# A transformer sandwich on one core: the last chunk's experts in pieces of two, one and one blocks

## The chip, the cores and the metric

The kernel runs on one core of a Trainium2 chip. Time is device microseconds of one execution; the number compared is the median over runs. The profile is one further execution, taken by the hardware profiler, with its own time.

## What is computed

Four sequences of 1024 tokens with 128 channels (fp32) pass through four residual layers, each `x = x + layernorm(layer(layernorm(x)))`: a linear recurrence (RWKV), a mixture of 16 experts, a delta-net attention, and last the layer this change is about:

```python
def _gqa(x, wq, wk, wv, wo):          # 16 heads of 8, 4 key heads, causal
...
    attn = jnp.where(causal, attn, jnp.float32(-jnp.inf))
    attn = jax.nn.softmax(attn, axis=-1)
    out = jnp.einsum('bhqk,bkhd->bqhd', attn, v).reshape(B, S, C)
    return out @ wo.T
def _moe(x, gate_w, expert_w):        # 8 experts, top 2, softmax of the two
    logits = t @ gate_w.T
    w, sel = jax.lax.top_k(logits, TOP_K)
...
    for e in range(N_EXPERTS):
        out = out + comb[:, e, None] * (t @ expert_w[e].T)
h = x + _gqa(_rmsnorm(x, attn_norm_w), wq, wk, wv, wo)
out = h + _moe(_rmsnorm(h, ffn_norm_w), gate_w, expert_w)
```

## The kernel before

Channels lie on the 128 partitions and tokens along the free axis, in chunks of 512 tokens (CH); a sequence is two chunks (NH) or eight blocks of 128 (NBLK). Stages A to C (the first three layers) run first, their later sequences interleaved with the last stage. The last stage is one long list written in the order in which the engines are to take it, with the scheduler switched off (`tc.manual_schedule()`): each engine works through its own instructions in just that order and waits where an operand isn't there.

The loop at the end walks over blocks (b, i), sequence by sequence. For each it issues units. A unit of `weighted` (L925) is one TensorE matmul of 128 keys against 4 heads by 128 queries (sc, L945, 512 columns), and its Exp on ScalarE (pr, L950); on the diagonal GpSimd masks pr (L954). Eight units behind, `products` (L937) multiplies four pr by the values into av, which holds 32 rows for each group of heads: eight sums, the denominator in row 8. Block i has 4(i + 1) such units. Between them lie the units of `maxima` of the block two ahead (matmul sm, L874 to L886, and a maximum on VectorE, L882 and L887), so the last two blocks, (3, 6) and (3, 7), with 28 and 32 units, have none beside them. The row maxima go into extra rows of qr by small DMAs (L909). sc has two PSUM banks (`scores`), sm three (`to_max`), av one.

After each unit comes `tick()`. A tick issues what is due, half a step of the work ahead (stage C and heads of the next sequences), and 0.65 step (PER_TICK_BEHIND) of the oldest generator in `behind_it`. A step is what a generator issues up to its next `yield`:

```python
        owed[1] = min(owed[1] + PER_TICK_BEHIND, 1.5)
        if behind_it and owed[1] >= 1.0:
            owed[1] -= 1.0
            if next(behind_it[0], True):
                behind_it.popleft()
```

These generators are `experts(b, h)`, one for each chunk, put there once its fourth block has its av. `finish` copies av (L964) to SBUF and stores its sums to DRAM (L971). `experts` first calls `project_out`: den and num come back from DRAM, heads spread over the partitions (L985, L986), Ln and Exp turn den into its reciprocal (L988, L989), GpSimd multiplies (L992), TensorE projects (wo, L997). Then rmsnorm (L526, L138, L120, L121, L1011), gate logits with tokens on partitions (L1016), top 2 on VectorE (L145 to L163, L1019 to L1029, L176 to L180), a transpose to 8 rows (comb, L1037), a store of them (row, L1044) and eight loads that spread each expert's row over 128 partitions (every, L1050). GpSimd forms n4 times gate for each expert (share, L1062), and TensorE adds the eight experts up (y, L1074), with the term of the residual centered ahead (L1057). Layernorm (L1076, L526, L138, L120, L121, L1081), residual (L1083), transposes back (L1088), the means (L1091) and the store of the output (L1094) follow. One such generator has about 80 steps. At the very end a loop of ticks drains what is left.

Of the kernel before, what the change touches and what calls it, by code (L numbers as in the profile page):

```python
# [11 lines left out]
FP = mybir.dt.float32  # L12
BF = mybir.dt.bfloat16
AF = mybir.ActivationFunctionType
# [4 lines left out]
P = 128  # L19
NB = 4  # L20
# [19 lines left out]
def sandwich(ctx: ExitStack, tc: tile.TileContext, x, vecs, cmats, rope, wa, wb, wc, wd, out):  # L40
# [73 lines left out]
    def chunk(h):  # L114
        return slice(h * CH, (h + 1) * CH)
# [20 lines left out]
    def project(pp, lhsT, rhs, name):  # L136
        ps = pp([P, CH], name)
        nc.tensor.matmul(ps, lhsT=lhsT, rhs=rhs, start=True, stop=True)  # L138
        return ps

    def topk(vals, nb, n_e, k, restart, pool):
# [21 lines left out]
        nc.vector.tensor_add(sel, sel, eq)  # L163
        return sel

    def restarts(nb, n_e, pool, name):
# [353 lines left out]
    def wait_for_it():  # L520
        for _ in range(LAG):
            yield

    def mean_square_steps(pp, src):
        sq = pp.scratch("rs")
        nc.scalar.activation(sq, src, AF.Square)  # L526
        yield
        yield
        ps = project(pp, mean, sq, "ln_v")
        yield  # L530
        return ps
# [393 lines left out]
    def weighted(b, i):  # L925
# [36 lines left out]
        def finish():  # L962
            av = pd.tile([P, CH], FP, tag="avs", name="av_sb")
            nc.scalar.copy(av, pavs.pop((b, i)))  # L964
            if i % 4 == 0:
                sums[b, i // 4] = dram.tile([4, 4, 9, CH], FP, tag="sums", name="sums")
            to = sums[b, i // 4].rearrange("g r d t -> g d r t")

            def stored():
                for g in range(4):  # L970
                    nc.sync.dma_start(out=to[g][:, :, tb], in_=r3(av[32 * g : 32 * g + 9, :], 4))  # L971
                if i % 4 == 3:
                    behind_it.append(experts(b, i // 4))

            later_on(4, stored)

        return [lambda j=j, g=g: unit(j, g) for j in range(i + 1) for g in range(4)]

    def project_out(b, h):

        n3, of = n3s[b, h], sums.pop((b, h))
        num = pd.tile([P, CH], FP, tag="share", name="num", bufs=3)
        den = pd.tile([P, CH], FP, tag="every", name="den", bufs=4)
        heads_of = of.rearrange("g r d t -> (g r) d t")
        nc.sync.dma_start(out=den, in_=heads_of[:, 8:9].to_broadcast([16, 8, CH]))  # L985
        nc.sync.dma_start(out=num, in_=heads_of[:, 0:8])  # L986
        yield from wait_for_it()
        nc.scalar.activation(den, den, AF.Ln)  # L988
        nc.scalar.activation(den, den, AF.Exp, scale=-1.0)  # L989
        yield  # L990
        yield
        nc.gpsimd.tensor_mul(num, num, den)  # L992
        yield
        yield
        yield
        po = room_f([P, CH], "wo_ps")
        nc.tensor.matmul(po, lhsT=wo_d, rhs=num, start=True, stop=True)  # L997
        nc.vector.tensor_add(n3, po, n3)
        yield

    def experts(b, h):

        yield from wait_for_it()
        yield from project_out(b, h)
        c = chunk(h)
        hT = n3s[b, h]
        n4 = pd.tile([P, CH], FP, tag="n4", name="n4", bufs=1)
        var = yield from mean_square_steps(room_f, hT)
# [4 lines left out]
        yield  # L1013
        pg = room_f([P, 4, 8], "gate_ps")
        for n in range(4):
            nc.tensor.matmul(pg[:, n, :], lhsT=n4[:, n * P : (n + 1) * P], rhs=wgate_d, start=True, stop=True)  # L1016
        yield
        lg = pd.tile([P, 4, 8], FP, name="lg")
        nc.vector.tensor_copy(lg, pg)  # L1019
        yield  # L1020
        sel = topk(lg, 4, 8, 2, restart8, pd)
        top = pd.tile([P, 4, 1], FP, name="top")
        nc.vector.tensor_reduce(top, lg, AX.X, ALU.max)
        nc.vector.tensor_sub(lg, lg, top.to_broadcast([P, 4, 8]))
        yield
# [3 lines left out]
        nc.vector.tensor_mul(sel, sel, lg)  # L1029
        normalized(sel, 4, 8, 0.0, pd)  # L1030
        yield
        yield
        yield

        pt = room_f([8, CH], "comb_ps")
        for n in range(4):
            nc.tensor.transpose(pt[:, n * P : (n + 1) * P], sel[:, n, :], ident)  # L1037
        yield
        comb = pd.tile([8, CH], FP, tag="last", name="comb", bufs=1)
        nc.scalar.copy(comb, pt)  # L1040
        yield
        yield
        row = dram.tile([8, CH], FP, tag="row", name="row")
        nc.sync.dma_start(out=row, in_=comb)  # L1044
# [3 lines left out]
        def spread_gate():  # L1048
            every = pd.tile([P, CH], FP, tag="every", name="every", bufs=4)
            nc.sync.dma_start(out=every, in_=row[len(gates)].partition_broadcast(P))  # L1050
            gates.append(every)
# [3 lines left out]
        yield from wait_for_it()  # L1055
        y = room_f([P, CH], "y")
        nc.tensor.matmul(y, lhsT=center, rhs=hT, start=True, stop=False)  # L1057
        shares = []

        def weigh():  # L1060
            shares.append(pd.tile([P, CH], FP, tag="share", name="share", bufs=3))
            nc.gpsimd.tensor_mul(shares[-1], n4, gates[len(shares) - 1])  # L1062
# [22 lines left out]
        yield  # L1085
        px = room_f([P, 4, P], "x_t")
        for j in range(4):
            nc.tensor.transpose(px[:, j, :], n4[:, j * P : (j + 1) * P], ident)  # L1088
        yield
        last = pd.tile([P, 4, P], FP, tag="last", name="last", bufs=1)  # L1090
        nc.vector.tensor_add(last, px, means[:, b, h * 4 : h * 4 + 4].unsqueeze(2).to_broadcast([P, 4, P]))  # L1091
        for _ in range(4):
            yield
        nc.sync.dma_start(  # L1094
            out=out[b, h * CH : (h + 1) * CH, :].rearrange("(n p) c -> p n c", p=P), in_=last,
        )
        yield

# [32 lines left out]

    coming = front()
    PER_TICK, PER_TICK_BEHIND = 0.5, 0.65
    owed = [0.0, 0.0]

# [4 lines left out]
    def tick():  # L1140
# [8 lines left out]
        if owed[0] >= 1.0:  # L1149
            owed[0] -= 1.0  # L1150
            advance()
        owed[1] = min(owed[1] + PER_TICK_BEHIND, 1.5)
        if behind_it and owed[1] >= 1.0:
            owed[1] -= 1.0
            if next(behind_it[0], True):
                behind_it.popleft()

    for h in range(NH):
# [13 lines left out]
    wexp = pd.tile([P, 8, P], FP, name="wexp", bufs=1)  # L1172
    nc.sync.dma_start(out=wexp, in_=wd[:, 328:].rearrange("p (e o) -> p e o", e=8))
    centered(wexp, 8, pd, "wmean")
    with tc.manual_schedule():
# [4 lines left out]
        for n, (b, i) in enumerate(blocks):  # L1180
# [9 lines left out]
            while (b, i) not in placed_rows:  # L1190
                tick()
            for u in units_of(n):
                u()
                tick()
        while held:
            held[0][0]()
            tick()
        while due or behind_it:
            tick()


def _constants():
# [13 lines left out]
    for p in range(P):  # L1216
        rope[p, 0] = cos[p % 4]
        rope[p, 1] = sin[p % 4] if p % 8 >= 4 else -sin[p % 4]
    return cmats, rope.reshape(P, -1)


def _arrays(i):

    cmats, rope = _constants()
    a = {n: np.asarray(v) for n, v in i.items()}
# [23 lines left out]
    def by_d(w):  # L1249
# [4 lines left out]
        by_d(a[F1 + "wq"].T), by_d(a[F1 + "wk"].T), a[F1 + "wv"].T, a[F1 + "wo"].T, a[F1 + "gate_w"].T,  # L1254
        a[F1 + "expert_w"].reshape(1024, P).T,
    ]
# [22 lines left out]
```

## Time and profile before

| | |
|---|---|
| runs, us | 1712.28, 1715.19, 1717.48; median 1715.19 |
| profiled execution, us | 1715.55, its span 1713.8 |
| busy, share of the span | PE 1310.6 (76%), DVE 1168.9 (68%), ACT 856.7 (50%), POOL 655.9 (38%) |
| last attention product (av) | starts at 1659.13, its copy at 1661.95 to 1662.54 |
| last store issued | 1710.60 |
| granted TensorE clock | 1.00 from 1600 to 1660, 0.68, 0.63 and 0.80 after it |

A line of the timeline is: start, duration, engine, source line, operation, out<-in with shapes, how many in a row were merged, and in brackets how long the engine had been idle and who ended that. An fp32 matmul appears as two passes (x2). PEld is the load of the weights. A line of the chain is: start, duration, engine, what. SPq rows are DMA issues on SyncE's queue.

### The profile page before, as it was taken

Reading aid. Unit: us, or ns where it says so; the run is one execution under the profiler, and the core shown is the slowest. Engines: PE = TensorE matmul, PEld = TensorE weight load, DVE = VectorE, ACT = ScalarE, POOL = GpSimd, SP = SyncE. Lnnn points to the kernel's source line nnn. Section 1 sums busy time; section 2 is a strip of 40 time slices with the busy share of each in tenths; the row PEclk is TensorE's granted clock in tenths of the full one; section 3 lists DMA queues with packets and bytes.
Section 4 is the critical chain, followed back from the end, with each engine's and each line's share of the span. In section 5 each row is a group of like instructions: output and inputs, shape, how many; then the busy total and the mean of one; then the engine's idle time right before and its main releaser. Section 6 shows DMA issues by size and latency. Waiting matters only on the chain.

```text
span 1713.8 us, 15167 instructions
## 1 busy us (share of the span) xinstructions
PE 1310.6 (76%) x4593; PEld 463.3 (27%) x4604; DVE 1168.9 (68%) x1991; ACT 856.7 (50%) x1565; POOL 655.9 (38%) x663
## 2 busy tenths in 40 slices
PE   2547887867865889678779869888887879889864
PEld 1213333312221323133223223322232223233311
DVE  4575676698775877867995597777779825577601
ACT  3457776624453457234436625645553345645561
POOL 5554353524252324323433363427227333122212
PEclk8669998978887999877779869987898669989996
DMA  2000110313033122101112111231113011110101
GB/s 97 13 7 6 25 50 25 96 40 108 13 111 110 53 65 85 44 12 34 45 58 70 53 57 54 70 92 46 38 37 101 21 48 64 45 61 29 54 22 56
DMA packets 59330, 90.49 MB, mean 53 GB/s; under 512 B 9904, under 2 KB 26800, under 8 KB 58544
## 3 DMA queue, kind: packets, MB, share of 16 engines
q1 hardware_dynamic: 59248, 89.52, 17.3%
q8 instruction: 36, 0.59, 0.1%
q14 instruction: 46, 0.38, 0.1%
HBM read 76.38 MB, written 12.71 MB: 52 GB/s over the span
## 4 chain that ended last, share of the span: by engine, by line
PE 32%; DVE 18%; ACT 6%; issue 4%; POOL 4%; DMA 2%; SPq 0%; POOLq 0%; DVEq 0%; ACTq 0%
PE av L937 8%; PE sc L945 5%; DVE ms L882 4%; DVE st L620 4%; ACT pr L950 3%; PE sm L874 3%; DVE ms L887 3%; PE y L1074 3%; PE sm L886 2%; PE ln_v L138 2%; PE num_ps L674 1%; POOL hid L473 1%; POOL share L1062 1%; PE sm L878 1%; PE g_ps L138 1%
## 5 line engine op out<-in xcount | busy, mean ns | idle before, releaser
L950 ACT ACTIVATE pr<-sc 128x512 f32<-128x512 f32 x576 | 328.2, 595 | 361.7 <-PE sc L945 358.0
L882 DVE TENSOR_REDUCE ms<-sm 128x1 f32<-128x512 f32 (+3 forms) x352 | 210.5, 633 | 114.2 <-PE sm L878 103.0
L945 PE MATMUL sc<-qr,keys_r 75*128 75x512 bf16 x576 | 234.1, 422 | 37.7 <-ACT pr L950 28.7
L887 DVE TENSOR_REDUCE ms<-sm 128x1 f32<-128x512 f32 x256 | 165.0, 682 | 56.4 <-PE sm L886 55.9
L937 PE MATMUL av<-pr,va 128*32 128x512 f32 x1152 | 183.1, 710 | 0.0
L954 POOL TENSOR_SCALAR_AFFINE_SELECT pr<-pr 128x512 f32<-128x512 f32 x128 | 89.4, 712 | 244.5 <-ACT pr L950 236.2
L874 PE MATMUL sm<-keys_r,qr 72*128 72x512 bf16 (+3 forms) x512 | 138.2, 337 | 46.3 <-DVE ms L882 43.9
L138 PE MATMUL ln_v<-rs,cm 128*128 128x512 f32 x176 | 113.0, 733 | 43.0 <-ACT rs L126 28.3
L473 POOL TENSOR_TENSOR hid<-hid,gate 128x512 f32<-128x512 f32 x64 | 81.9, 1280 | 162.9 <-DVE hid L468 124.6
L614 POOL TENSOR_TENSOR kv<-vrep,phi 128x512 f32<-128x512 f32 x64 | 85.6, 1342 | 115.0 <-issue 47.9
L1062 POOL TENSOR_TENSOR share<-n,every 128x512 f32<-128x512 f32 x64 | 87.2, 1373 | 91.1 <-DMA every<-row 70.5
L455 PE MATMUL y_ps<-hid,wbt 128*128 128x512 f32 x144 | 84.1, 669 | 46.3 <-DVE hid L474 44.4
L886 PE MATMUL sm<-keys_r,qr 72*128 72x512 bf16 x256 | 99.6, 417 | 25.0 <-DVE ms L887 20.6
L945 PEld LDWEIGHTS <-keys_r 75*128 75x128 bf16 x576 | 58.7, 106 | 153.2 <-issue 126.3
L878 PE MATMUL sm<-later,identb 128*128 128x128 bf16 (+2 forms) x341 | 90.5, 265 | 0.0
L474 DVE TENSOR_TENSOR hid<-hid,g 128x512 f32<-128x512 f32 x72 | 57.7, 801 | 46.7 <-POOL hid L473 39.9
L138 PE MATMUL u_ps<-n,wbt 128*128 128x512 f32 x144 | 77.3, 618 | 7.6 <-DVE hid L468 5.1
L138 PE MATMUL g_ps<-n,wbt 128*128 128x512 f32 x144 | 78.8, 630 | 3.7 <-DVE hid L463 1.6
L1074 PE MATMUL y<-share,wexp 128*128 128x512 f32 x128 | 70.8, 644 | 9.6 <-POOL share L1062 9.4
L874 PEld LDWEIGHTS <-qr 72*128 72x128 bf16 x512 | 51.0, 107 | 99.4 <-issue 82.8
L465 ACT ACTIVATE g<-hid 128x512 f32<-128x512 f32 x72 | 45.1, 626 | 55.4 <-DVE hid L463 55.3
L674 PE MATMUL num_ps<-st,cm 128*32 128x512 f32 x128 | 52.5, 777 | 25.7 <-DVE st L637 25.5
(300 smaller groups left out, 2394.9 us busy)
## 6 DMA issues: line engine op xcount, KB each, us to landing
gate<-rows SPq DMA_DIRECT2D x64, 256.0 KB
vrep<-v_rows SPq DMA_DIRECT2D x64, 256.0 KB
every<-row SPq DMA_DIRECT2D x64, 256.0 KB
qr<-dq SPq DMA_DIRECT2D x72, 128.0 KB
turn<-in_rope_dram SPq DMA_DIRECT2D x8, 512.0 KB
dq<-qp SPq DMA_DIRECT2D x8, 384.0 KB
keys_r<-dk SPq DMA_DIRECT2D x72, 32.0 KB
sums<-av_sb SPq DMA_DIRECT2D x128, 18.0 KB
```

What stands on the lines that cost most here:

```text
L138: nc.tensor.matmul(ps, lhsT=lhsT, rhs=rhs, start=True, stop=True)
L473: nc.gpsimd.tensor_mul(a, a, gate)
L874: nc.tensor.matmul(view[:, k, :], lhsT=qr[0:KROWS, h, tb], rhs=kr[0:KROWS, half, h // 4, 0:n_s], start=(k == 0), stop=False, skip_group_ch ...
L878: nc.tensor.matmul(view[:, :, n_s - P :], lhsT=identb, rhs=later[:, :in_bank, :], start=False, stop=True, skip_group_check=True,)
L882: nc.vector.tensor_reduce(ms[:, 0, h0 : h0 + in_bank], view, AX.X, ALU.max)
L886: nc.tensor.matmul(sc, lhsT=qr[0:KROWS, h, tb], rhs=kr[0:KROWS, 0, h // 4, :], start=True, stop=True)
L887: nc.vector.tensor_reduce(ms[:, 1, h : h + 1], sc, AX.X, ALU.max)
L937: nc.tensor.matmul(pavs[b, i][32 * g : 32 * g + 32, :], lhsT=va[:, j, g, :], rhs=pr, start=(j == 0), stop=(j == i),)
L945: nc.tensor.matmul(sc, lhsT=kr[0:ROWS, j // 4, g, j % 4 * P : (j % 4 + 1) * P], rhs=qr[0:ROWS, 4 * g : 4 * g + 4, tb], start=True, stop=True,)
L950: nc.scalar.activation(pr, sc, AF.Exp)
L1062: nc.gpsimd.tensor_mul(shares[-1], n4, gates[len(shares) - 1])
L1074: nc.tensor.matmul(y, lhsT=wexp[:, e, :], rhs=shares[e], start=False, stop=(e == 7))
```

## The change

Only the last chunk, blocks 4 to 7 of sequence 3, is treated in another way.

- Blocks 4 and 5 go through `experts` as one piece of 256 tokens; every tile of the generator is cut to `wide = nb * P` columns. It is put into `behind_it` after block 5.
- Blocks 6 and 7 (`LAST`) each have their own generator `last_block`, of 128 tokens, which every tick advances by one step, whatever the rate. It works without DRAM: eight matmuls with a new 0/1 constant `pick` lay the numerators and denominators of the heads out over the partitions; TensorE spreads a gate row with a matmul of a one-hot row block (`space["one"]`) against comb; VectorE multiplies four experts at once out of PSUM; shares are the stationary side and the expert weights the moving one, so that y has tokens on its partitions, the sum of squares comes from ScalarE's Square itself, and no transposes are needed at the end. x is transposed back and the means added ahead of that.
- `last_block` takes its PSUM tiles from `to_max`, and y from `scores`. Its SBUF lies in the buffer of qr of the chunk that is done.
- In sequence 3, blocks 4 to 7, the generators behind run at 1.0, 1.0, 2.0 and 2.0 steps a tick instead of 0.65.
- The constants `pick` (128 x 304 fp32) are appended to the weights and loaded once, behind wexp.

```diff
+                if (b, i) in LAST:
+                    later_on(1, lambda: ends.append(last_block(b, i, av)))
+                    return
...
-                if i % 4 == 3:
-                    behind_it.append(experts(b, i // 4))
+                if i % 4 == 3 or (b, i + 1) in LAST:
+                    behind_it.append(experts(b, i // 4, i % 4 + 1))
...
+    LAST = {(NB - 1, NBLK - 2), (NB - 1, NBLK - 1)}
+    def last_block(b, i, av):
+        if not space:
+            space["all"] = pe.tile([P, 32, P], FP, tag="qr", name="space")
+            space["one"] = space["all"][0:8, 24:32, :]
+            nc.vector.tensor_copy(space["one"], ident[0:8, 0:8].unsqueeze(2).to_broadcast([8, 8, P]))
...
+        px = to_max([P, P], "x_t")
+        nc.tensor.transpose(px, xT[b][:, c], ident)
+        parts = to_max([P, 2, P], "parts_ps")
+        for m in (1, 0):
+            for r in range(4):
+                nc.tensor.matmul(
+                    parts[:, m, :], lhsT=pick[:, m, 24 - 8 * r : 24 - 8 * r + P], rhs=av[:, r * P : (r + 1) * P],
+                    start=(r == 0), stop=(r == 3), skip_group_check=True,
+                )
+        nc.vector.tensor_scalar_add(xfin, px, means[:, b, i : i + 1])
+        yield
+        nc.scalar.activation(den, parts[:, 1, :], AF.Ln)
+        nc.scalar.activation(den, den, AF.Exp, scale=-1.0)
+        yield
+        nc.vector.tensor_mul(num, parts[:, 0, :], den)
+        yield
+        po = to_max([P, P], "wo_ps")
+        nc.tensor.matmul(po, lhsT=wo_d, rhs=num, start=True, stop=True)
+        yield
+        nc.vector.tensor_add(hT, po, hT)
...
+        nc.vector.scalar_tensor_tensor(n4, hT, vec("ffn_norm_w"), rs, op0=ALU.mult, op1=ALU.mult)
+        yield
+        pg = to_max([P, 1, 8], "gate_ps")
+        nc.tensor.matmul(pg[:, 0, :], lhsT=n4, rhs=wgate_d, start=True, stop=True)
...
+        nc.tensor.transpose(pt, sel[:, 0, :], ident)
+        yield
+        comb = den[0:8]
+        nc.scalar.copy(comb, pt)
+        yield
+        y = scores([P, P], "y")
+        nc.tensor.matmul(y, lhsT=hT, rhs=center, start=True, stop=False)
+        for m in range(2):
+            every = to_max([P, 4, P], "every_ps")
+            for e in range(4):
+                nc.tensor.matmul(every[:, e, :], lhsT=space["one"][:, 4 * m + e, :], rhs=comb, start=True, stop=True)
+            yield
+            nc.vector.tensor_mul(shares[m], every, n4.unsqueeze(1).to_broadcast([P, 4, P]))
+            yield
+        for e in range(8):
+            nc.tensor.matmul(y, lhsT=shares[e // 4][:, e % 4, :], rhs=wexp[:, e, :], start=False, stop=(e == 7))
+            if e % 4 == 3:
+                yield
+        stat = own.tile([P, 1, 1], FP, name="stat")[:, 0, :]
+        nc.scalar.activation(num, y, AF.Square, accum_out=stat)
+        rstd(stat, eps5, scale=1.0 / P)
+        yield
+        nc.vector.scalar_tensor_tensor(xfin, y, stat, xfin, op0=ALU.mult, op1=ALU.add)
+        yield
+        nc.sync.dma_start(out=out[b, c, :], in_=xfin)
...
+    RATES = 1.0, 1.0, 2.0, 2.0
...
-        owed[1] = min(owed[1] + PER_TICK_BEHIND, 1.5)
-        if behind_it and owed[1] >= 1.0:
+        owed[1] = min(owed[1] + at_rate[0], 1.5 * max(at_rate[0], 1.0))
+        while behind_it and owed[1] >= 1.0:
             owed[1] -= 1.0
             if next(behind_it[0], True):
                 behind_it.popleft()
+        for steps in list(ends):
+            if next(steps, True):
+                ends.remove(steps)
...
+            if b == NB - 1 and i >= NBLK // 2:
+                at_rate[0] = RATES[i - NBLK // 2]
```

## The prediction

> **What bounds the kernel now.** I read the busy time by stage over the last 100 us first, then the chain that ended last, then the timeline of the same stretch. By stage:
>
> ```profile
> 1620.00:1640.00 20.00, 17.11 (x86) 4.82 (x87) 1.60 (x3) 15.17 (x29) 3.75 (x6) 1.00 0.01 1
> 1640.00:1660.00 20.00, 15.68 (x84) 3.34 (x84) 0.00 (x0) 15.49 (x29) 1.58 (x3) 1.00 0.07 18
> 1660.00:1680.00 20.00, 6.85 (x20) 2.18 (x14) 1.44 (x2) 3.72 (x6) 2.08 (x3) 0.68 0.11 30
> 1680.00:1700.00 20.00, 11.45 (x24) 5.14 (x23) 2.88 (x19) 0.80 (x2) 8.25 (x7) 0.63 0.30 106
> 1700.00:1714.00 14.00, 4.98 (x12) 1.61 (x10) 1.38 (x2) 2.46 (x4) 2.92 (x3) 0.80 0.07 19
> ```
>
> Columns: stretch, length, busy PE, PEld, DVE, ACT, POOL, granted TensorE clock, DMA share, GB/s. Until 1660 TensorE and ScalarE are both some 80% busy. After that nothing is: one thing waits for another. The chain says for what:
>
> ```profile
> 1659.20 2.73 PE av L937 x16
> 1663.60 1.53 DMA sums<-av_sb
> 1665.33 3.39 DMA den<-sums
> ...
> 1686.36 1.46 DMA row<-comb
> 1687.83 3.09 DMA every<-row
> 1691.06 1.72 POOL share L1062 x2
> ...
> 1696.01 3.12 DMA every<-row
> ```
>
> The last attention sum ends at 1662, and then a whole four-block chunk goes through the experts alone, with two trips through DRAM (sums to den, row to every). From the av copy at 1661.95 to the span's end at 1713.8 are **51.85 us**, in which only this chain counts. The timeline gives its prices and those of the stretch ahead of it:
>
> ```profile
> 1623.45 1.02 PE L1074 MATMUL y<-share,wexp 128*128 128x512 f32 x2
> ...
> 1654.40 0.60 PE L945 MATMUL sc<-qr,keys_r 75*128 75x512 bf16 x2
> 1654.82 2.15 ACT L950 ACTIVATE pr<-sc 128x512 f32<-128x512 f32 x4 [0.72 <-PE sc L945]
> ...
> 1661.95 0.59 ACT L964 COPY av_sb<-av 128x512 f32<-128x512 f32 x1 [2.11 <-PE av L937]
> ...
> 1671.42 2.07 PE L997 MATMUL wo_ps<-num,wdt 128*128 128x512 f32 x2 [9.51 <-POOL num L992]
> ...
> 1709.88 0.69 DVE L1091 TENSOR_TENSOR last<-x_t,means 128x512 f32<-128x512 f32 x1 [2.55 <-PE x_t L1088]
> 1710.60 0.39 SPq L1094 DMA_DIRECT2D out_dram<-last  x1
> ```
>
> A quiet cycle of four units takes 2.87 us (sc pairs at 1651.53, 1654.40, 1657.27): ScalarE works 2.15 of it and waits 0.72. The same fp32 product over 512 columns takes 1.02 us at full clock and 2.07 in the tail. At full clock it holds TensorE's queue for 0.86 (the sc behind y starts at 1624.31), so 0.43 for 256 columns and 0.215 for 128; the rest of the 1.02, 0.17, is draining.
>
> **Part 1, the tail.** Blocks 4 and 5, and block 6, leave it; only block 7 (128 tokens) remains. Prices: an ACT instruction costs 0.23 at 32 columns (L1026) and 0.63 at 512, so about 0.31 at 128; DVE 0.19 and 0.69, so 0.29; a dependent fp32 matmul over 128 columns 0.215 and 0.17 to drain, 0.38 at full clock, 0.78 at half. A hop between engines costs 0.03 to 0.05 (1673.49 to 1673.53). Matmuls that change weights are load-bound: eight passes of gate_ps took 1.06 at full clock, 0.13 each.
> - av copy 0.64. Eight matmuls with pick, 16 passes: 2.2 if a load (0.12) runs beside the pass before it (0.107), 3.6 if the two add. The nearest row, the y matmuls of L1074, has its loads under the passes, so I take 2.3, at full clock since TensorE has just been dense. Ln and Exp 0.7, product 0.34: 4.0 in place of the trip to 1671.42 (9.5).
> - wo, add, square, ln_v, Ln and Exp, n4, gate: 0.41+0.34+0.36+0.41+0.71+0.37+0.43 = 3.0.
> - Top-k: 3.5 us before (1681.13 to 1684.65) with four MAX8 and 32 columns; with one MAX8 and the Exp beside it about 3.1.
> - comb transpose and copy 0.7; the first four spreading matmuls 1.2; two DVE products 0.74 each, with 0.3 between them; the last four y matmuls 1.2. That is 4.9, in place of row, eight every loads, eight POOL products and sixteen passes (1684.70 to 1702.8, 18.1).
> - Square with a sum (not in the trace; nearest row 0.31, taken 0.38, at most 0.6), two one-column ACT 0.46, the last DVE step 0.34, store 3.0 (1710.57 to 1713.8 is 3.2 for four times the bytes). The mean's matmul, the POOL add and the last transposes go.
>
> Sum 19.2 at full clock. At half clock from wo on, add 0.4 for wo and ln_v each, 0.35 gate, 0.2 comb, 1.15 first spread, 1.0 between the products, 1.15 y: 23.8. Which one? Row first: in the tail of before every matmul up to 1693 ran at half, gaps of 1.4 us included, but it entered cold after 9.5 us of idling. The Trainium skill ("TensorE: Matmul & The Clock Gate", What's actually happening) has the gate cool only after about an idle window of 3.4 us. By the rule matmuls up to gate stay warm and those after top-k (3.1 us plus its neighbours) are cold: 22.7. By the row all are: 23.8. I take **23** (19 to 26, the top with serial weight loads). Saved: 51.85 - 23 = **28.9** (26 to 32.7).
>
> **Part 2, what blocks 6 and 7 must now carry.** Their 60 units ran from 1612.06 to 1659.2, 47.1 us; fifteen quiet cycles would be 43.1, so the work put between them cost 4.0. That work was six y matmuls, ln_v and x_t (6.5 us of TensorE), four ACT steps (2.5) and two av copies (1.2), 10.2 in all: 39% showed. The new load:
> - Piece of two blocks, which runs at two steps a tick here: TensorE 12 matmuls of 256 columns at 0.43, gate 0.5, transposes 0.4, together 6.1; ACT nine at 0.42, lg 0.2, comb 0.4, together 4.4.
> - Block 6 alone: TensorE 30 matmuls of 128 columns (8 pick, 8 spreading, 9 y, wo, ln_v, gate, and the transposes x_t and comb), mostly load-bound at 0.24, 6.7 in all; ACT 2.8 (five at 0.31, the Square, four small).
> - av copies 1.2. Sum **21.2**.
>
> At 39% this shows as 8.3, all of it would be 21.2. Two reasons for more than 39%. y of block 6 takes one of the two score banks: the built order has eight sc in a row that wait for the Exp just before, one of them for the last DVE step. A single-bank unit costs sc latency 0.42 + 0.55 + 0.07 = 1.04 against 0.72, 0.33 times 8 = 2.6, partly filled by the eight spreading and eight y matmuls. And two steps a tick put at most one sc between a step and the next that needs it (wo, add, square, ln_v: 1.1 us of hops). TensorE's queue then stands with the next sc behind it, and ScalarE runs dry. I take 55% and 2 us for the bank: 13.7, so **+9.7** over the 4.0 of before (+4.3 to +17).
>
> DVE (1.6 us busy of 1620 to 1640) and POOL hide their parts; without that cover POOL's eight half products are 5 us. Gates of the piece: first share 5.3 us after comb before (1685.76 to 1691.06); eleven steps at two a tick are some 4.5 us, so the first wait is perhaps 1 us, inside the 55%. SP: den, num come ahead of block 7's qr<-mt, which can cost it 3 us; block 7 starts 28 units later.
>
> **Part 3, blocks 4 and 5.** The rate goes from 0.65 to 1.0 and takes in the 9.0 us that left blocks 6 and 7. At 39% 3.5, less where DVE sets the pace (16.10 busy of 20 at 1580 to 1600): **+2.4** (0 to 5). The pick load (156 KB, without a wait, behind wexp at 710) is nothing; if not, 1.4 us, wexp's issue.
>
> Sum: -28.9 + 9.7 + 2.4 = -16.8. The profiled execution is 1715.55 (span 1713.8 and 1.75 around it), 0.36 over the median of 1715.19; I subtract from the median: **1698**.
>
> **Rivals.**
> - *The load hides as before* (39%, bank filled): +4.3 + 1, tail 21: 1715.2 - 30.9 + 5.3 = 1690. For it: quiet TensorE time of 1.1 us a cycle. Against: the waits above.
> - *Load-bound and cold*: weights never overlap, tail 26, load 80% shown (+13) and +4: 1715.2 - 25.9 + 17 = 1706. For it: gate_ps.
> - *Slower, one mechanism*: TensorE's in-order waits in blocks 6 and 7. Some 23 steps there wait for another engine (14 in the piece: wo, two ln_v, gate, comb, eight shares, x_t; 8 in block 6: pick, wo, ln_v, gate, comb, spreading, twice y; one sc behind y). If each drains both score banks, 0.42 for the next sc and a hop of 1 us, it costs 1.4: 23 times 1.4 = 32 over the plain time, 28 more than before: with +2.4 and -28.9 about 1717; with +5 in blocks 4 and 5 and a tail of 26, 1722. It decides from about 1.3 us a wait. Against: the eight such steps of before cost 4.0 together, 0.5 each.
> - *It doesn't do what it says*: the piece could spill past block 7. The built order has its last transposes ten units before the end, so hardly.
>
> **Chances.** Forecast (1694 to 1703) 0.55, hidden 0.20, load-bound 0.15, slower or level 0.10. 0.3% is 5 us, about what a measurement of this kernel can tell from no change: level is 1710 to 1720. The last case is split over level (0.05) and slower (0.05); a slice of the load-bound one, 0.02, goes over 1710, half to each. Faster 0.88, same 0.06, slower 0.06. Range 1688 to 1708.
>
> **What would show it.** In the changed profile: no DMA between the last av copy and the store; 23 us from that copy to the end, wo at 0.4 or 0.8 us telling the clock; the pick matmuls in 2.3 or 3.6; the DVE stretch of top-k at 3.1; 60 units of blocks 6 and 7 in 57 us, with the idle time of ScalarE before pr largest in the eight units around y. I am wrong if these 60 units take over 75 us, or if blocks 4 and 5 grow by more than 5.

## The result and the profile after

The changed kernel takes 1734.95 us (median of 7 runs, 1725.58 to 1739.65) against 1717.48 of the kernel before on the same chip (7 runs, 1712.28 to 1730.57): a ratio of 1.0089, 95% interval 1.0065 to 1.0114. It is **slower by 0.9%, some 17 us**, where I forecast 17 us faster. The profiled execution took 1731.29, with a span of 1729.6.

Single executions of one kernel differ by 10 us and more, mostly in the long part ahead of the last four blocks. So I cut both spans at the ACT copies that end an attention block (av_sb out of av) and compare the stages. Where the code is the same and the clock is full, a stage repeats to 0.1 us (block 7 takes 22.0 or 22.1 in three kernels). Below full clock it does not: block 6 of the changed kernel took 28.8 us at 0.68, and the same instructions in c_y_bank (below) 24.0 at 1.00. Each row is one execution. First the kernel before by stage, the rows being blocks 4, 5, 6 and 7 (the tail behind them, 51.8, is in the prediction); columns as in the prediction (length, busy PE, PEld, DVE, ACT, POOL, granted clock, DMA share, GB/s):

```profile
1557.80:1585.20 27.40, 24.17 (x119) 8.72 (x119) 21.97 (x41) 14.79 (x26) 4.99 (x6) 0.88 0.12 33
1585.20:1615.70 30.50, 26.82 (x134) 9.62 (x133) 23.76 (x54) 15.63 (x31) 8.70 (x10) 0.94 0.21 69
1615.70:1639.90 24.20, 20.84 (x102) 5.92 (x102) 3.95 (x5) 17.97 (x33) 7.25 (x8) 1.00 0.04 9
1639.90:1662.00 22.10, 17.69 (x92) 3.75 (x91) 0.00 (x0) 15.59 (x30) 2.39 (x4) 1.00 0.07 16
```

The kernel after, the same four stages, its tail, and twenty quiet microseconds out of block 6:

```profile
1559.00:1596.50 37.50, 30.11 (x126) 10.46 (x126) 25.41 (x61) 15.46 (x30) 5.01 (x6) 0.72 0.11 34
1596.50:1638.40 41.90, 38.87 (x138) 12.41 (x138) 20.89 (x36) 16.74 (x30) 13.84 (x13) 0.74 0.16 50
1638.40:1667.20 28.80, 25.44 (x98) 6.05 (x96) 4.23 (x21) 17.92 (x37) 3.45 (x5) 0.68 0.09 26
1667.20:1707.70 40.50, 32.99 (x171) 16.02 (x170) 6.39 (x25) 19.77 (x44) 8.77 (x13) 0.87 0.08 22
1707.70:1729.60 21.90, 11.72 (x58) 10.22 (x58) 5.35 (x23) 3.41 (x12) 0.00 (x0) 0.75 0.01 3
1640.00:1660.00 20.00, 18.52 (x67) 4.22 (x65) 2.75 (x15) 11.12 (x22) 0.73 (x1) 0.57 0.07 18
```

The tail did what was forecast: 51.8 became 21.9, 29.9 less. The four blocks ahead of it gave back more than that: 104.2 became 148.7, **44.5 more**, where I had 12.1. With 1.2 us of difference ahead of block 4 that is the whole change of the span: 1.2 + 44.5 - 29.9 = 15.8 = 1729.6 - 1713.8. Read the clock column beside the lengths: before, 0.88, 0.94, 1.00, 1.00; after, 0.72, 0.74, 0.68, 0.87. The clock records hold 1.00 and 0.50 and nothing between, so a stage of length L at a mean clock c spent 2 x (1 - c) x L at half clock: 6.6 + 3.7 = 10 us of these blocks before, 21.0 + 21.8 + 18.4 + 10.5 = 72 us after.

What half a clock costs is seen in the chain that ended last, kernel after. The two av rows are quiet units at the end of block 5 and in block 6, two cycles apart; the last line belongs to the tail, where the two trips through DRAM of before have no successor:

```profile
1636.37 1.99 PE av L947 x8
1645.05 1.87 PE av L947 x8
...
1718.39 3.71 PE every_ps L1187 x16
```

and in the timeline of the kernel after, a step of such a cycle, PE and ACT:

```profile
1642.62 1.03 PE L955 MATMUL sc<-qr,keys_r 75*128 75x512 bf16 x2
...
1643.32 1.09 ACT L960 ACTIVATE pr<-sc 128x512 f32<-128x512 f32 x2 [2.04 <-PE sc L955]
```

Two cycles take 1645.05 - 1636.37 = 8.68, 4.3 each, against 2.87 at full clock in the prediction's rows. An sc pair takes 1.03 instead of 0.60, and the engine that waits is now ScalarE (2.04 us for sc). The bound has moved: at full clock ScalarE works 2.15 us of a cycle and waits 0.72, at half clock it is TensorE that hardly pauses. So each microsecond at half clock loses 1 - 2.87/4.3 = 0.33. This is an estimate, from quiet cycles; by it 62 more of them lose some **20 of the 44.5 us**. And the row 1640 to 1660 shows that a high busy share alone does not bring the clock back at once: TensorE is recorded busy 18.52 of 20 us there, and runs at 0.57.

The waits that come with the drops stand in the timeline of the kernel after, PE alone (idle time and its releaser in brackets):

```profile
1575.03 1.98 PE L1010 MATMUL wo_ps<-num,wdt 128*128 128x512 f32 x2 [1.45 <-POOL num L1005]
...
1589.61 1.01 PE L1051 MATMUL comb_ps<-ident,sel 128*8 128x128 f32 x4 [2.64 <-DVE sel L190]
...
1622.14 0.65 PE L1102 MATMUL x_t<-ident,n 128*128 128x128 f32 x4 [1.95 <-POOL n L1097]
```

Each is a step of the experts that stands in TensorE's queue before its operand is there; in these two blocks an x_t (1.77 for POOL, at 1560.73) and a gate (1.33 for DVE, at 1582.60) belong to them too, 9.1 us in all five. (The kernel before has two such waits in these blocks, 1.82 and 2.22, and a drop behind each.) The comb wait lies behind its drop, at 1585.4, which followed the gate's. The wo matmuls after their wait take 1.98 for two passes. The last line lies ahead of the slow stretch: the clock records show half clock from 1622.9 to 1657.1, **34 us after a wait of 1.95**.

The clock changes on a grid. In all fourteen traces of this case every stretch at 1.00 or at 0.50, but for those that the ends of a trace cut off, is a whole number of windows of 3.41 us; in the changed kernel 34.1, 30.7 and 10.2 us (10, 9 and 3) follow one another from 1622.94 on. So the window into which a wait falls counts. Four of them, kernel after, two ahead of that drop, the first behind it, and the last at half clock:

```profile
1616.12:1619.53 3.41, 2.65 (x13) 0.75 (x13) 1.90 (x4) 1.95 (x5) 0.00 (x0) 1.00 0.00 0
1619.53:1622.94 3.41, 1.46 (x12) 0.78 (x9) 1.99 (x4) 1.00 (x2) 1.26 (x1) 1.00 0.00 0
1622.94:1626.36 3.42, 3.42 (x12) 0.97 (x14) 3.10 (x5) 2.16 (x4) 0.00 (x0) 0.50 0.25 77
1653.66:1657.08 3.42, 3.22 (x11) 0.85 (x11) 0.10 (x1) 1.94 (x5) 0.00 (x0) 0.50 0.00 0
```

TensorE is recorded busy 1.46 of 3.41 us in the window ahead of the drop. Counted over all windows of the fourteen traces: a full-clock window recorded busy under 40% was followed by half clock every time (399 of 399), one of 50 to 70% in 205 of 685 cases, one of 90% and more never (0 of 2131). The way back is harder: a half-clock window under 70% was never followed by full clock (0 of 758), one of 90% and more in 728 of 1074 cases. The same wait of 1.95 at the same x_t was followed by 10.2 us of half clock in c_y_bank and d_defer6: how long it lasts is not set by the wait.

The tail itself, timeline of the kernel after:

```profile
1708.36 2.05 PE L1135 MATMUL parts_ps<-av_sb,pick 128*128 128x128 f32 x16 [0.42 <-ACT av_sb L974]
...
1711.45 0.49 PE L1147 MATMUL wo_ps<-space,wdt 128*128 128x128 f32 x2 [1.03 <-DVE space L1144]
...
1717.58 0.38 PE L1177 MATMUL comb_ps<-ident,sel 128*8 128x128 f32 x1 [2.88 <-DVE sel L190]
...
1718.32 3.78 PE L1187 MATMUL every_ps<-space 8*128 8x128 f32 x16
1722.02 3.62 PE L1192 MATMUL y<-wexp,space 128*128 128x128 f32 x16
```

No DMA is left between the copy and the store. Pick takes 2.05 for 16 passes, so its weight loads do run beside the passes; wo takes 0.49, near the warm price; after top-k the matmuls are at half clock (3.78 and 3.62 for 16 passes).

### The profile page after: what moved, and what is told of

Same layout as the page of the kernel before. It is cut to its first block, busy times and chain, and to the rows that moved or that the text cites. A ratio compares the mean times of both kernels' runs of the same rounds, so it can differ in the third digit from the quotient of the medians.

```text
span 1729.6 us, 15448 instructions
## 1 busy us (share of the span) xinstructions
PE 1338.3 (77%) x4701; PEld 481.5 (28%) x4712; DVE 1179.1 (68%) x2036; ACT 860.2 (50%) x1587; POOL 652.9 (38%) x663
## 4 chain that ended last, share of the span: by engine, by line
PE 35%; DVE 19%; ACT 6%; issue 4%; POOL 2%; DMA 1%; SPq 0%; POOLq 0%; DVEq 0%; ACTq 0%
PE av L947 9%; PE sc L955 6%; DVE st L630 4%; DVE ms L892 4%; PE y L1088 3%; DVE ms L897 3%; PE sm L884 3%; PE sm L896 3%; ACT pr L960 3%; PE ln_v L138 2%; POOL hid L483 1%; PE num_ps L684 1%; PE sm L888 1%; PE g_ps L138 1%; ACT ln_v L120 1%
## 5 line engine op out<-in xcount | busy, mean ns | idle before, releaser
L955 PE MATMUL sc<-qr,keys_r 75*128 75x512 bf16 x576 | 242.5, 436 | 35.4 <-ACT pr L960 26.4
L947 PE MATMUL av<-pr,va 128*32 128x512 f32 x1152 | 195.3, 749 | 0.0
L138 PE MATMUL ln_v<-rs,cm 128*128 128x512 f32 (+1 forms) x176 | 111.4, 724 | 43.2 <-ACT rs L126 29.4
L1076 POOL TENSOR_TENSOR share<-n,every 128x512 f32<-128x512 f32 (+1 forms) x64 | 82.0, 1292 | 68.4 <-DMA every<-row 33.1
L1088 PE MATMUL y<-share,wexp 128*128 128x512 f32 (+1 forms) x128 | 66.3, 600 | 0.9 <-POOL share L1076 0.7
```

The source lines that it names most:

```text
L947: nc.tensor.matmul(pavs[b, i][32 * g : 32 * g + 32, :], lhsT=va[:, j, g, :], rhs=pr, start=(j == 0), stop=(j == i),)
L955: nc.tensor.matmul(sc, lhsT=kr[0:ROWS, j // 4, g, j % 4 * P : (j % 4 + 1) * P], rhs=qr[0:ROWS, 4 * g : 4 * g + 4, tb], start=True, stop=True,)
L1088: nc.tensor.matmul(y, lhsT=wexp[:, e, :], rhs=shares[e], start=False, stop=(e == 7))
```

## The experiments

**Theories.** *Clock*: a TensorE wait of one or two microseconds in a busy stretch drops the clock, the half clock then outlasts the wait, and blocks 4 to 7 pay 0.33 us for each microsecond of it. *Load*: TensorE simply has more work and more waits than the attention can hide; the clock only accompanies that. *Single bank*: y of block 6 takes one of two score banks, and block 7 pays for that. The edits below leave out what only passes a variable on. Every count of half-clock time comes from the stage rows as above.

### The rates alone, and the change without them

a_rates_only is the kernel before with nothing but the faster pace:

```
+    RATES = 1.0, 1.0, 2.0, 2.0
...
-        owed[1] = min(owed[1] + PER_TICK_BEHIND, 1.5)
-        if behind_it and owed[1] >= 1.0:
+        owed[1] = min(owed[1] + at_rate[0], 1.5 * max(at_rate[0], 1.0))
+        while behind_it and owed[1] >= 1.0:
...
+            if b == NB - 1 and i >= NBLK // 2:
+                at_rate[0] = RATES[i - NBLK // 2]
```

> The kernel before with the new rates alone (1.0, 1.0, 2.0, 2.0 steps a tick in the last four blocks), no pieces. Clock theory (the time is lost in half-clock windows that waits of TensorE bring on): blocks 4 and 5, together 57.9 us before and 79.4 after, grow by 10 or more with half-clock windows in them, blocks 6 and 7 lose about 4; about 1725. Load theory (only added work and waits count): the same work is moved, +2.4 in blocks 4 and 5 and -4 in 6 and 7; about 1716.

b_late_rates is the change with `RATES = 0.65, 0.65, 2.0, 2.0`.

> The changed kernel with 0.65, 0.65, 2.0, 2.0 in place of 1.0, 1.0, 2.0, 2.0. Clock theory and load theory both: blocks 4 and 5 go back to about 58 us if the rate is what lengthened them; blocks 6 and 7 take the rest of the first chunk's experts, +4 to +8 over the 69 us after; about 1718 to 1722. If something else than the rate lengthened blocks 4 and 5, about 1735.

Measured: a 1733.83, 1.0075 [1.0051, 1.0099]; b 1725.45, 1.0026 [0.9989, 1.0063]. Blocks 4 and 5 of a, by stage:

```profile
1561.00:1600.30 39.30, 33.32 (x125) 11.27 (x125) 25.20 (x61) 15.52 (x29) 5.07 (x6) 0.66 0.11 33
1600.30:1637.80 37.50, 34.16 (x138) 11.07 (x138) 20.69 (x36) 16.51 (x30) 13.70 (x13) 0.86 0.17 56
```

76.8 us against 57.9: going from 0.65 to 1.0 steps a tick is enough for nearly all that the change lost there, in a kernel whose tail is the old one. a gets 3.6 us back in block 6 (20.6 against 24.2), as that block has less to carry. b keeps blocks 4 and 5 at 58.8, but pays in blocks 6 and 7, which come to 78.6 us with 43 us of half clock: the same steps, later. So the pace alone makes the loss of blocks 4 and 5, and slowing it alone only moves it.

### The score bank, and block 6 left to the tail

c_y_bank gives y another bank; d_defer6 holds back the steps of block 6's own end until attention is over, so both last blocks run them in the tail and only the piece of two blocks is left in blocks 6 and 7.

```
c:
-        y = scores([P, P], "y")
+        y = room_f([P, P], "y")
d:
-    ends = []
+    ends, deferred = [], [True]
...
-        for steps in list(ends):
+        for steps in list(ends) if len(ends) == 2 or not deferred else []:
...
+            if not due:
+                deferred.clear()
```

> The changed kernel with y of the single blocks in the other small pool of PSUM banks, so that the scores keep both of theirs. If the single score bank is the cost, block 7 (40.5 us after, 22.0 before) falls by 8 or more and the time to about 1726. If not, within 3 us of the changed kernel's 1735.

> The changed kernel with block 6's own steps held back until block 7's begin, so that both run side by side in the tail and block 7's attention carries only the piece. Load theory: block 7 loses 12 to 15 of its 18.5 us of growth, the tail grows from 21.9 by 4 to 6; about 1726. Clock theory: the same sign, but the size goes with the half-clock windows left between 1620 and 1700: about 1722 if block 7 stays at full clock.

Measured: c 1728.03, 1.0035 [1.0012, 1.0057]; d 1724.68, 1.0026 [1.0002, 1.0049]. Block 7 of c takes 40.5 us, exactly as in the changed kernel: by the stage rows **the single bank is not what makes block 7 long**. It spent 17 us at half clock there against 10, worth 2.1 at 0.33, so that the 2 us or so that I had charged for the bank may be hidden in it; the other 12 or more are not the bank's. The time of c is a miss, though: 1728 is near the 1726 that I had set for the bank, and its interval lies clear of the change's. In the two traces the difference stands in block 5 (37.7 against 41.9) and block 6 (24.0 against 28.8), which run the same instructions in both, at different clocks. Why the median moved is open. Blocks 6 and 7 of d, by stage (its tail is 31.1):

```profile
1627.50:1651.60 24.10, 18.45 (x98) 4.93 (x96) 3.64 (x20) 17.87 (x37) 3.21 (x5) 1.00 0.11 32
1651.60:1677.90 26.30, 21.72 (x113) 7.03 (x113) 1.43 (x3) 17.29 (x33) 8.71 (x13) 1.00 0.11 31
```

Block 6's own steps are worth 40.5 - 26.3 = 14.2 us in block 7 (3.5 of them by half clock, at 0.33) and 31.1 - 21.9 = 9.2 in the tail: dearer beside attention than alone. The piece of two blocks by itself, at full clock, costs only 24.1 + 26.3 - 46.3 = 4.1 over the kernel before. The tail grew by more than the 4 to 6 that I expected of it.

### Waits put in by hand

Two kernels put waits into blocks 6 and 7 of the kernel before: a product on another engine, then a TensorE transpose of it, whose values are used nowhere.

```
+                if b == NB - 1 and i >= 6 and k in (8, 20):
+                    wait = pe.tile([P, CH], FP, tag="whole", name="wait", bufs=1)
+                    nc.gpsimd.tensor_mul(wait[:, :512], held[-1][3][:, :512], held[-1][3][:, :512])
+                    nc.tensor.transpose(to_max([P, P], "wait_ps"), wait[:, :P], ident)
```

e_long_waits is this (two waits a block, on POOL); f_short_waits has four a block, at `k in (4, 11, 18, 25)`, with 128 columns on VectorE.

> The kernel before with four made-up waits of TensorE in its last two blocks: GpSimd squares the newest pr (128x512) and TensorE transposes a piece of it, in units 8 and 20 of each; the values are used nowhere. Each should hold TensorE for some 2 us. Clock theory: each of them is followed by two or more half-clock windows; blocks 6 and 7, together 46.2 us before, grow by 18 or more, with at least 20 us at half clock. Load theory: by the waits alone, 8 to 9, and the clock stays at full.

> As the long waits, but eight of about 1 us or less: VectorE squares 128 columns of the newest pr, in units 4, 11, 18 and 25 of each of the last two blocks. Clock theory: no half-clock window, so blocks 6 and 7 grow by at most the sum, 4 to 8 us, less than with the long waits though their sum is near it. Load theory: the same growth as with the long waits, 8 to 9.

Measured, one run each: e 1741.4, f 1730.76. One of e's waits, PE timeline:

```profile
1643.68 0.39 PE L945 MATMUL sc<-qr,keys_r 75*128 75x512 bf16 x1
1645.96 0.33 PE L1197 MATMUL wait_ps<-ident,wait 128*128 128x128 f32 x1 [1.89 <-POOL wait L1196]
1646.13 0.60 PE L945 MATMUL sc<-qr,keys_r 75*128 75x512 bf16 x2
...
1647.69 0.63 PE L945 MATMUL sc<-qr,keys_r 75*128 75x512 bf16 x1
```

The matmul just behind the wait still runs fast (an sc pair in 0.60); a microsecond or two later a single sc takes 0.63 where it took 0.39. Blocks 6 and 7 of e by stage, and then block 7 of f:

```profile
1626.30:1657.00 30.70, 24.50 (x104) 6.46 (x105) 3.98 (x5) 18.22 (x33) 9.31 (x10) 0.89 0.03 7
1657.00:1688.60 31.60, 24.91 (x94) 4.67 (x93) 0.00 (x0) 15.90 (x30) 4.52 (x6) 0.68 0.04 11
```

```profile
1643.60:1677.70 34.10, 28.86 (x96) 5.06 (x95) 1.17 (x4) 16.08 (x29) 2.42 (x4) 0.55 0.04 11
```

e: four waits of 1.86, 1.89, 1.86 and 1.80, 7.4 us, lengthened the two blocks by 62.3 - 46.3 = 16.0, where I had set 18 or more for the clock and 8 to 9 for the load. With 6.8 + 20.2 = 27.0 us of half clock at 0.33, 8.9, the clock theory gives 16.3; the waits alone give half of what was measured. Three of the four waits left a window of 3.41 us busy 45 to 50%, and half clock followed in the next; ahead of the third wait the drop was already under way (the clock fell 0.45 us into it, behind a window busy 64%). This is the plainest case, though a single run: almost no work added, and half clock costs as much as the wait.

f missed what I expected by either theory. Its waits came out longer than meant (1.50, 0.19, 1.78, 2.45, 1.10, 0, 1.01, 1.08: 9.1 us), so it isn't the test of short waits that it was to be. Block 7, with waits of 1.0 to 1.1, ran at 0.55: 31 of 34 us at half clock. That the waits held it there is not shown, as the changed kernel stayed at half clock from 1622.9 to 1657.1 with no wait over 0.54. 37 us of it in both blocks at 0.33 and 9.1 of waits would be 21.3; 18.4 were measured.

### TensorE kept busy ahead of the waits

If the clock is the matter, useless work in the gaps should make the kernel faster. cover() issues fp32 matmuls into a spare bank ahead of wo, gate, comb and x_t; what they compute is used nowhere.

```
+    def cover(hT):
+        if at_rate[0] == 1.0:
+            for _ in range(2):
+                nc.tensor.matmul(to_max([P, CH], "cover"), lhsT=center, rhs=hT, start=True, stop=True)
...
+        cover(hT)
```

g_covered is a_rates_only with this. j_after_covered is the whole change with it (one product where the rate is 2.0, and one ahead of block 6's ln_v and comb).

> The kernel with the new rates alone, and two idle fp32 products of 512 columns (0.86 us each at full clock) put ahead of the wo, gate, comb and x_t matmuls while the rate is 1.0, so that TensorE works where it waited 1.3 to 2.6 us; their values are used nowhere. Clock theory: the half-clock windows in blocks 4 and 5 (37.6 us of them) mostly go and the two blocks, 76.8 us, fall to about 65 though 8 us of work are added; about 1722. Load theory: they stay or grow, 77 to 84; about 1735 to 1740.

> The changed kernel as it is, with idle fp32 products of 512 columns (two at rate 1.0, one at 2.0) ahead of wo, gate, comb and x_t of the pieces, and one ahead of ln_v and comb of block 6; their values are used nowhere. Clock theory: half-clock windows in blocks 4 to 7, 71.6 us, fall to 20 or less, and the time falls to about 1720 although some 13 us of TensorE work are added. Load theory: 1735 or more.

Measured: g 1724.49, 1.0038 [1.0017, 1.0058] where a had 1.0075; j 1718.62, 1.0002 [0.9978, 1.0026] where the change had 1.0089. Blocks 4 and 5 of g, by stage:

```profile
1558.40:1590.90 32.50, 29.36 (x142) 11.71 (x143) 24.86 (x61) 15.12 (x29) 5.02 (x6) 1.00 0.11 29
1590.90:1625.60 34.70, 31.68 (x143) 11.00 (x143) 20.33 (x36) 16.42 (x30) 13.58 (x13) 1.00 0.20 71
```

Twenty passes of nothing (8.6 us at 0.43) took these blocks from 76.8 to 67.2 us, and the clock from 0.66 and 0.86 to 1.00. Load can't explain that more work takes less time. **The clock theory holds for blocks 4 and 5.** j does the same for the change: 32.5 + 34.7 + 24.7 in blocks 4 to 6, all at 1.00, against 37.5 + 41.9 + 28.8. But its block 7 stays at 40.5, clock 0.87. That stage has another cause, and d names whose steps they are.

### Steps that are asked for earlier

h_defer6_lead is d with a pause ahead of each waiting matmul, so that its operand is there when TensorE comes to it. i_slow_lead is h with `RATES = 0.65, 0.65, 2.0, 2.0`. k_lead_cover is h with one cover() after each pause.

```
+    def lead():
+        for _ in range(3 if at_rate[0] == 1.0 else 2 if at_rate[0] == 2.0 else 0):
+            yield
...
+        yield from lead()
```

> The changed kernel with block 6's own steps held back to the tail, and with three empty steps (two at rate 2.0) ahead of the wo, gate, comb and x_t matmuls of the pieces, so that what they wait for is there. Clock theory: blocks 4 and 5 (76.8 us) fall to about 60 to 64 and blocks 6 and 7 stay near 50; the tail 31; about 1708. Load theory: no gain over 1725, since the same work is done.

> The changed kernel with block 6 held back to the tail, the old rate of 0.65 in the first two of its four blocks, 2.0 in the last two, and the two empty steps ahead of the matmuls that waited. Clock theory: blocks 4 and 5 near the 58.8 us that the old rate gave, blocks 6 and 7 near 52 to 58 with few half-clock windows, tail 31: about 1703, below both kernels. Load theory: the load that leaves blocks 4 and 5 comes back in 6 and 7 in full (78.7 us there with the late rates alone): about 1720.

> The fastest so far (block 6 held back to the tail, empty steps ahead of the waiting matmuls, new rates) with one idle fp32 product of 512 columns more ahead of each of those matmuls. Clock theory: the 27 half-clock us left in blocks 5 and 6 go, blocks 4 to 7 fall from 117.8 to about 112; about 1702. Load theory: 8 products of 0.86 us each on top, about 1712.

Measured: h 1706.84, 0.9945 [0.9921, 0.9969]; i 1716.38, 1.0004 [0.9977, 1.0031]; k 1710.28, 0.9931 [0.9897, 0.9966]. h and k are faster than the kernel before. Their blocks 4 to 7 sum to 117.8 and 116.7 (d 127.2), half clock in them 31 and 7 us (d 37), tails 30.9 and 32.0. h's pauses took away the long waits of block 4 but not all of block 5's (40.7 us, 17 of them at half clock), so blocks 4 and 5 came to 67.0 where I had set 60 to 64. i missed: I thought the old pace with pauses the safest, at about 1703, and it came nearer to the 1720 of the load theory. Its blocks 4 and 5, with the same steps as b's, took 63.1 us (b 58.8). Then a wait for an Exp at the turn of block 5 to 6 came ahead of a drop at 1623.1 (an x_t waited 1.19 for POOL just behind it); PE timeline of i:

```profile
1622.58 0.38 PE L961 MATMUL sc<-qr,keys_r 75*128 75x512 bf16 x1 [1.43 <-ACT pr L966]
```

Its block 6 took 33.6, 20.5 of them at half clock. k fell less than I had set for it: 116.7 us, not 112, and a time near the 1712 of the load theory. Its nine covers are themselves 7.7 us of work.

### Block 6's steps spread out

Is it the work of block 6's own steps that costs 14 us in block 7, or how densely they stand? l_block6_slower is j with these steps at every second tick:

```
-        for steps in list(ends):
+        for steps in list(ends) if not held or now[0] % 2 else []:
```

> The changed kernel with covers, and with block 6's own steps on every second tick while block 7's attention runs, so that its spreading and its y matmuls fall into the tail. If the density of its steps (waits of one engine on another within a tick) is what lengthens block 7, 40.5 us with and without covers, block 7 falls to 31 or less and the tail grows by at most 5: about 1713. If its work is what counts, block 7 falls only by the work that leaves it, some 5 us, and the tail gives that back: about 1718 as before.

Measured: **1708.15, 0.9924 [0.9900, 0.9948]**, faster than the kernel before and, where the change itself had 1.0089, 1.6% under that; the intervals of h, k and l overlap, so they are not told apart. Block 7 of j by stage (its tail is 22.2), then block 7 and the tail of l:

```profile
1644.50:1685.00 40.50, 34.93 (x177) 16.23 (x176) 6.39 (x25) 19.79 (x44) 8.84 (x13) 0.87 0.08 22
```

```profile
1640.70:1669.60 28.90, 26.30 (x143) 11.23 (x142) 4.45 (x22) 18.67 (x40) 8.81 (x13) 1.00 0.10 29
1669.60:1694.80 25.20, 16.07 (x92) 14.29 (x92) 6.88 (x26) 4.17 (x16) 0.00 (x0) 0.79 0.02 5
```

11.6 us leave block 7 and 3.0 come into the tail. At every second tick the steps don't all fit: 34 of 177 matmuls move into the tail, about half of what block 6's end has, while of the other engines' work nearly all stays (22 of 25 on DVE, 40 of 44 on ACT). So part of the 11.6 is work that went elsewhere: 4.1 at the 0.12 a pass of a weight load beside it, 8.2 at the 0.24 of a load-bound pass. The clock, back at 1.00, is 10.5 us of half clock less, 3.5. By the first price 4 us are left for the spacing itself, by the second none. TensorE's idle time in the block, length less busy, speaks for the first: 5.6 us in j, 2.6 in l. In the waits of block 7 the line that tells it is ScalarE's for its scores (us in total, times, longest). The kernel before, then after:

```profile
ACT pr L950 <- PE sc L945: 4.3, 6, 0.7
ACT pr L960 <- PE sc L955: 16.3, 12, 2.7
```

and l:

```profile
ACT pr L966 <- PE sc L961: 6.8, 8, 2.0
```

So of the 18.4 us that block 7 grew by, 12.0 are ScalarE running dry, because its scores come late. By the stage rows TensorE is recorded busy for 15.3 us more in the changed block 7 and idle for 3.1 more (7.5 against 4.4): the scores stand mostly behind the added passes and their half clock, and less behind TensorE's own waits (1.38 at ln_v and 1.58 at comb are the longest).

## Why the prediction was wrong

- **Tail, 51.85 to 23: right.** 21.9 measured; 29.9 saved, 28.9 forecast. Pick 2.05 (2.3), wo 0.49 (0.41), top-k 2.8 from the copy of the gates at 1714.74 to the transpose comb (3.1), both spreading groups together 3.78 and both y groups 3.62 at half clock. Where rule and row were weighed against each other, the rule did better: warm until the gate, cold after top-k, which gave 22.7; the row's "all cold" gave 23.8.
- **Part 3, blocks 4 and 5, +2.4 (0 to 5): wrong, +21.5.** This is the step that failed first. I counted 9.0 us of extra work at 39%, and the clock not at all, though the row of block 4 before already stood at 0.88. Half-clock time grew from 10 to 43 us; at 0.33 that is 10.7, an estimate. TensorE's idle time there, length less busy, grew by 3.5 (6.9 to 10.4), as the kernel before waits too. a_rates_only, c and d have the same steps in these blocks and took 76.8 to 76.9 us, so some 2.5 of the 21.5 belong to this execution. g_covered keeps the clock at 1.00 and lands at 67.2 with 8.6 us of useless passes in it, so the load costs between 0.7 and 9.3 over the 57.9 of before.
- **Part 2, blocks 6 and 7, +9.7: wrong by size, +23.0** (46.3 to 69.3). 29 us at half clock make 9.5 of it, by the estimate of 0.33; that term was missing. The 13.5 left are near my 9.7, but that is partly luck, as they are differently made up: the piece of two blocks costs 4.1 at full clock (d), block 6's own steps 14.2 in block 7. And the hiding failed: I let 45% of the load vanish in idle time, but TensorE's idle time in the two blocks did not shrink, it grew from 7.8 to 10.9 us. The 2 us for the single score bank were neither confirmed nor refuted (c, whose clock was lower in that block). That 55% of the load shows was a share of work alone; l shows that the same steps thinned out, with half of their matmuls left to the tail, cost 11.6 us less there and 3.0 more in the tail.
- **Warm and cold priced only where I thought of it.** I asked about the clock in the tail and took full clock for the rest, because the rows of blocks 6 and 7 before said 1.00. They said so of a stream whose longest wait is 0.82 (block 6); the change puts longer waits into it. The rule of the Trainium skill that served in the tail ("TensorE: Matmul & The Clock Gate", What's actually happening: cool after an idle window of about 3.4 us, warm again after as long a busy one) would have let me do the same here, as no wait in these blocks is that long. There the measurement differs from it: waits of 1.3 to 2.6 us came with half clock, windows of 3.41 us recorded busy under 40% were enough for a drop, and half clock outlasted 18.5 us of recorded work in 20.
- **Rivals.** The "slower" one, TensorE's in-order waits, came nearest in time: 1717 to 1722, where 1715.2 and the measured 17.5 make 1733. That is in part luck: it put 23 waits of 1.4 into blocks 6 and 7, where two of the measured ones reach 1.3 (1.38 and 1.58), and left blocks 4 and 5, where five do, at 2.4 to 5. And it counted each wait once, where e's waits of 1.85 cost four each. Its 0.05 was too little: "the eight such steps of before cost 0.5 each" was read in blocks 6 and 7 at a pace of 0.65. *Load-bound and cold* fell (pick 2.05), *hidden as before* fell, nothing spilled past block 7. Of my two signs of being wrong, one came: the 60 units took 71 us (57 forecast, 75 the limit), but blocks 4 and 5 grew by far more than 5.

What stays open: which half-full windows drop the clock (about a third of those recorded busy 50 to 70% did), and why a window of 90% and more brings it back in some cases only. In the changed kernel's block 7 waits of 1.38 and 1.58 at 1679.95 and 1685.09 lie in or beside windows busy 56 to 66%, and the drop came at 1687.8. How the 14.2 us of block 6's steps in block 7 divide is an estimate too: 58 passes more at 0.12 are 7.0, half clock 3.5, idle TensorE 2.9; no run takes them apart.

## What to carry to other kernels

Before steps are pushed into a stream that keeps TensorE busy, count, beside their work, the matmuls among them that will wait, and price each such wait at its length plus a third (here) of the half-clock time that follows (10.2 us behind the last wait of e, 34.1 behind the wait of 1.95 above). Do not count on idle time of the stream to hide the work: here it did not shrink. Ask for the operand some ticks ahead, space the steps so that every other engine finishes before TensorE arrives, or, where neither can be done, put a spare matmul in front: the same change went from 0.9% slower to 0.8% faster by spacing and spare matmuls alone. A long serial tail may still be worth shortening, but what moves out of it must be added up where it lands, at the clock that it will find there.

## What the hardware showed that I had not expected

- The clock changes only at the borders of a grid of 3.41 us, between 1.00 and 0.50, and went with how busy TensorE was recorded in the window before. At full clock, windows recorded busy under 40% were followed by half clock in 399 of 399 cases, those of 90% and more in none of 2131 (fourteen traces). A wait of one or two microseconds can be enough: three of the four hand-made waits of 1.8 to 1.9 left a window busy 45 to 50%, and the next had half clock (e).
- Recorded busy time brings the clock back only in part of the cases: 18.52 of 20 us busy at a granted clock of 0.57 (after, 1640 to 1660), while a like stream of attention units in the kernel before kept 1.00 at 17.69 of 22.1 (block 7). The same stream can live at either clock, according to how it came in.
- Useless TensorE work paid: 20 spare passes took 9.6 us off two blocks (a to g).
